# Bringing the late edges to their columns as three bf16 digits: one step of a graph attention and expert kernel on one Trainium2 core

## The chip, the core and the metric

The kernel runs on one core of one Trainium2 chip. The time is the device time of one execution in microseconds. The core's engines run side by side, each in its own order: TensorE (PE; PEld is its weight load), VectorE (DVE), ScalarE (ACT), GpSimd (POOL) and SyncE (SP, which issues DMA). Where one needs another's result it waits on a semaphore.

## The reference: what is computed

The program is a graph attention layer over 6250 nodes and 100,000 edges, followed by a feed-forward layer with eight experts of which each node uses one. Cut to what matters:

```python
# attention: x (6250, 256), 2 heads of 128
Wh = (layernorm(x) @ W_w + W_b).reshape(N, 2, 128)
s, t = Wh . a_src, Wh . a_dst                       # one number per node and head
e = leaky_relu(s[src] + t[dst], 0.2)                # one number per edge and head
alpha = softmax of e over the edges of one src
x = x + segment_sum(alpha * Wh[dst], src)           # Wh where a node has no edge
# experts: W1 (256, 1024), Wd (8, 1024, 256)
h = gelu(layernorm(x) @ W1 + b1)
probs = softmax(h @ Wg + bg); pick the best expert e of each node
x = x + probs[e] * (h @ Wd[e] + bd[e])
```

The edges come unsorted by `src`, so each node's edges must first be found, and then the rows `Wh[dst]` fetched from memory.

## The kernel before

**Prologue (to about 114 us).** The edges are sorted as keys on DVE. A key holds the source node, the destination (13 bits, from bit 8) and the node's place in its block (the low 8 bits). PE projects the nodes (L456), and their rows go to a table in DRAM, which ACT's queue stores. POOL sets small constants at the start.

**Blocks.** The 6250 nodes are 49 blocks of 128 (`NB`), one node to a partition. Each block gathers its edges' rows as 14 columns (`T`) of 128 rows. Eight columns (`ND`) hold the first eight edges of each node directly. Edges beyond the eighth are the *late* edges: up to 32 per node (`NR`), packed over the block into 768 slots (`NS`), that is six more columns (`NC`). Edges to the most frequent destinations, the *hot* pairs, go another way, without a gather.

The steps of one block b that matter here:

- `window`: POOL fetches each node's stretch of sorted keys (L619) into `win`.
- `measure`: DVE counts each node's edges; ACT makes `over`, the number of late ones (L640).
- `prefix`: PE adds `over` up over the partitions (L650). `prefix_out`: ACT copies the result to `late` (L653): a node's first slot in column 0, the slot after its last in column 2. It copies the first slot to the last column of `rest` as well (L655).
- `split`: DVE takes the window apart. The late keys (21 bits of each) become fp32 numbers in `rest`, 2^23 plus the bits (L659). `pick` is 1 where a slot (of 768) belongs to the node (L662, L663). L666 to L674 make the places and pairs.
- `gather_late`: six PE products (L738) of `pick`, 128 slots at a time, with `rest`, 33 columns. Each slot has one node, so the product brings that node's 32 late keys and its first slot to the slot.
- `choose`: DVE subtracts the first slot from the slot's number (L745), so knows which of the 32 keys is the slot's, takes it (L747 to L751), and cuts destination and place out of its bits (L753, L755, and L756 on ACT).
- `spread` transposes the places (PE L761, ACT L763), and SP sends them through DRAM (`lrow`) back to all partitions (`lbc`). `compare` (DVE L771) and `factors` (PE L779) make the attention's source factors from it.
- `fetch`: POOL issues the 14 gathers of table rows (L792), in three groups.
- `compare_back` (DVE L809), `weigh` (DVE L821 to L823, ACT L824 and L826) and `add_up` (PE L833) give each row its weight and add the rows of a node up in PSUM. `finish` (DVE) divides.

**Expert phases.** After every four blocks the feed-forward layer runs for their nodes: hidden layer (PE L920, ACT L922), choice of expert, turned rows (PE L1043, ACT L1044 and L1059) that POOL sends to their expert (L1064), and expert products (PE L1154).

**The order** is written out by hand. Each step is put with `at(slot, place, step, block)`, three slots to a block (`u = 3 * b`). The plan is sorted by slot and place, and each engine runs its instructions in the order in which the sorted steps issue them. Several blocks are under way at a time: a block's `split` stands at slot u-3, its `fetch` from u on, its `add_up` from u+3 on. `split` stands at place 12 of its slot, `weigh` of another block at place 8.751, `gather_late` at 33.7.

Of the kernel before, what the change touches and what calls it, by code (L numbers as in the profile page):

```python
# [10 lines left out]
F32 = mybir.dt.float32  # L11
BF16 = mybir.dt.bfloat16
I32 = mybir.dt.int32
U16 = mybir.dt.uint16
AF = mybir.ActivationFunctionType
ALU = mybir.AluOpType
# [7 lines left out]
P = 128  # L24
# [12 lines left out]
def common_path(  # L37
# [22 lines left out]
    nc = tc.nc  # L60
# [19 lines left out]
    HB, HK = 2, 4  # L80
    HOT = HB * P
    ND, NC, WIN = 8, 6, HK + 40
    NR = WIN - HK - ND
    KS = ES + WIN
    NS = NC * P
# [25 lines left out]
    const = ctx.enter_context(tc.tile_pool(name="const", bufs=1))  # L111
# [47 lines left out]
    first = const.tile([P, NB + 1], I32, name="first")  # L159
    minus_nd = const.tile([P, 1], F32, name="minus_nd")  # L160
    nc.gpsimd.memset(minus_nd, float(-ND))
    iota_bf = const.tile([P, HOT], BF16, name="iota_bf")
    nc.vector.tensor_copy(iota_bf, iota_s[:, :HOT])

# [3 lines left out]
    late = const.tile([P, NB, 3], F32, name="late")  # L168
# [4 lines left out]
    bias = const.tile([P, C], F32, name="bias")  # L173
# [20 lines left out]
    with ExitStack() as edges:  # L194
# [3 lines left out]
        def at(slot, place, fn, *args):  # L198
            plan.append((slot, place, len(plan), fn, args))

        kp = edges.enter_context(tc.tile_pool(name="keyp", bufs=2))
# [122 lines left out]
        bufs = [None] + [keyb if i % 2 == 0 else keya[:, :ES] for i in range(len(steps))]  # L324
# [204 lines left out]
        for f0, f1, t0, step in ((n0, n1, 8.0, 0.7), (n4, NB - 1, 15, 2.0)):  # L529
            for j, b in enumerate(range(f0, f1)):  # L530
                c = b % CH
# [81 lines left out]
        win, kept, rows, own, sums, res = {}, {}, {}, {}, {}, {}  # L613
# [37 lines left out]

        def prefix_out(b):
            nc.scalar.copy(late[:, b, :], kept[b].pop("po"))  # L653
            rest = kept[b]["rest"] = kp.tile([P, NR + 1], F32, name="rest")
            nc.scalar.copy(rest[:, NR:], late[:, b, 0:1])  # L655

        def split(b):
            w = win.pop(b)
            nc.vector.tensor_scalar(kept[b]["rest"].bitcast(I32)[:, :NR], w[:, HK + ND:], 0x1FFFFF, 0x4B000000,  # L659
                                    op0=ALU.bitwise_and, op1=ALU.bitwise_or)  # L660
            pick = kp.tile([P, NS], F32, name="pick", bufs=1)
            nc.vector.tensor_scalar(pick, iota_s, late[:, b, 0:1], None, op0=ALU.is_ge)  # L662
            nc.vector.scalar_tensor_tensor(pick, iota_s, late[:, b, 2:3], pick, op0=ALU.is_lt, op1=ALU.mult)  # L663

            place_i = kp.tile([P, HK + ND], I32, name="place_i")
            nc.vector.tensor_single_scalar(place_i, w[:, :HK + ND], 255, op=ALU.bitwise_and)  # L666
            loc = kp.tile([P, T], F32, name="loc", bufs=5)
            nc.vector.scalar_tensor_tensor(loc[:, :ND], iota_r[:, :ND], cnt[:, b:b + 1], place_i[:, HK:],
                                           op0=ALU.is_lt, op1=ALU.mult)

            hot_i = kp.tile([P, HK], I32, name="hot_i")
            nc.vector.tensor_single_scalar(hot_i, w[:, :HK], 8, op=ALU.logical_shift_right)
            pair = kp.tile([P, HK], F32, name="pair")
            nc.vector.tensor_scalar(pair, hot_i, float(0x400000 + (b << 13)), None, op0=ALU.subtract)  # L674
            kept[b].update(loc=loc, pick=pick, pair=pair, place=place_i)

        def pick_pairs(b):
            pair, place_i = kept[b].pop("pair"), kept[b].pop("place")
            d, p = kept[b]["both"] = [kp.tile([P, HK, w], BF16, name=n, bufs=1) for n, w in (("dests", HOT), ("places", P))]
            for r in range(HK):  # L680
                nc.vector.tensor_scalar(d[:, r, :], iota_bf, pair[:, r:r + 1], None, op0=ALU.is_equal)  # L681
            nc.vector.tensor_tensor(p, iota_bf[:, P:2 * P].unsqueeze(1).to_broadcast([P, HK, P]),
                                    place_i[:, :HK].unsqueeze(2).to_broadcast([P, HK, P]), op=ALU.is_equal)
# [49 lines left out]
        def gather_late(b):  # L733
            k = kept[b]
            k["pm"] = ps2.tile([P, 512], F32, name="pm")
            pk = k["pm"][:, :NC * (NR + 1)].rearrange("p (c r) -> p c r", c=NC)
            for c in range(NC):
                nc.tensor.matmul(pk[:, c, :], k["pick"][:, c * P:(c + 1) * P], k["rest"], start=True, stop=True)  # L738

        def choose(b):  # L740
            k = kept[b]
# [182 lines left out]
        def blocks_of(k):  # L924
            return range(max(0, (k - 1) * FB + 1), min(NB, k * FB + 1))
# [272 lines left out]
        for b in range(NB):  # L1198
            u = 3 * b
            at(u + -6, 64.258, window, b)  # L1200
            at(u + -4, 24, measure, b)
            at(u + -4, 50.755, prefix, b)
            at(u + -3, 5, prefix_out, b)
            at(u + -3, 12, split, b)
            at(u + -3, 33.7, gather_late, b)
            at(u + -2, 62.758, pick_pairs, b)
            at(max(u + -1, -0.2), 63, load_terms, b)
            at(u + 1, 18.756, scale_terms, b, 0)
            at(u + 2, 4.751, scale_terms, b, 1)
            at(u + 0, 51.019, count_pairs, b)  # L1210
            at(u + 2, 51, weigh_pairs, b)
            at(u + 4, 51.256, add_pairs, b)
            at(u + -2, 16, choose, b)
            at(u + -2, 33.5, spread, b)
            at(u + 0, 9, compare, b)
            at(u + 0, 33, factors, b)
            at(u + 1, 47, factor_sums, b)
            at(u + 5, 42.752, owned, b)
            at(u + 6, 13, owned_biased, b)
            for q in range(3):  # L1220
                at(u + 0 + q, 30, fetch, b, q)
                at(u + 1 + q, 51.259, compare_back, b, q)
                at(u + 2 + q, 8.751, weigh, b, q)
                at(u + 3 + q, 32, add_up, b, q)
            at(u + 6, 14, finish, b)

        worked = n_off = 0
        u = [3 * blocks_of(k)[-1] + 6 for k in range(NPH)]
# [57 lines left out]
@with_exitstack  # L1286
def gat_then_ffn_kernel(
    ctx: ExitStack,
    tc: tile.TileContext,
    x: bass.AP,  # L1290
    src: bass.AP,
    dst: bass.AP,
    W: bass.AP,
    Wb: bass.AP,
    a: bass.AP,
    W1: bass.AP,
    b1: bass.AP,
    Wg: bass.AP,
    bg: bass.AP,
    Wd: bass.AP,  # L1300
    bd: bass.AP,
    out: bass.AP,
):
    keep = ctx.enter_context(tc.tile_pool(name="keep", bufs=1))
    odd = keep.tile([1, 1], I32, name="odd")
    common_path(tc, x, src, dst, W, Wb, a, W1, b1, Wg, bg, Wd, bd, out, odd)
    flag = tc.nc.values_load(odd[0:1, 0:1], min_val=0, max_val=1,
                             skip_runtime_bounds_check_because="a flag, 0 or 1")
    with tc.If(flag > 0):
        general_path(tc, x, src, dst, W, Wb, a, W1, b1, Wg, bg, Wd, bd, out)  # L1310
# [506 lines left out]
```

## Time and profile before

| | us |
|---|---|
| median of 3 runs | 1271.98 (1270.6 to 1276.46) |
| the profiled execution | 1270.99 |
| its span, first to last instruction | 1268.9 |
| PE busy | 1108.0 (87%) |
| DVE busy | 969.4 (76%) |
| ACT busy | 677.6 (53%) |
| POOL busy | 835.5 (66%) |
| mean granted PE clock | 0.948 of full speed |

The profile is of one execution. A group's line gives line, engine, operation, the tiles out<-in, and a count; after the bar busy time and the mean of one in ns; after the next bar the idle time of the engine just before these instructions and what ended it. `issue` is idle time for which the profile shows no release. A timeline line begins with start and duration in us, with the idle time before it in brackets. A chain line has start, duration and the work; a line of waits has the total, how often, and the longest. "Slices" are 40 equal parts of the span, a digit being busy tenths. L numbers are lines of the kernel before.

### The profile page before, as it was taken

To read this page: it belongs to the slowest core of one execution; us is meant where nothing else is said; L and a number is where in the kernel's file an instruction comes from. 1 tells how busy PE (TensorE), PEld (TensorE's weight loads), DVE (VectorE), ACT (ScalarE), POOL (GpSimd) and SP (SyncE) were. 2 spreads that over 40 slices of the span, in tenths; PEclk is the share of its full clock that TensorE was granted. 3 is DMA by queue.
4 is the path that set the end of the run, shared out by engine and by line. 5 is a ranking of instruction groups with operands and counts; after the bars stand their busy time and mean duration, and the time that the engine had idled before them with its cause. 6 is when DMAs were issued, how large, how long until landed. Compare 5 with 4: busy or idle time off the path is not lost.

```text
span 1268.9 us, 22698 instructions
## 1 busy us (share of the span) xinstructions
PE 1108.0 (87%) x6551; PEld 864.0 (68%) x6551; DVE 969.4 (76%) x3509; ACT 677.6 (53%) x2011; POOL 835.5 (66%) x941
## 2 busy tenths in 40 slices
PE   4685677697888989999989999999999999999994
PEld 3464565566566677786876867868678687685784
DVE  6986889888979789798897997979979979753110
ACT  4684344555646447556474665655745647555221
POOL 1003777777777777777777777777777777736551
PEclk9797688898998989999999999999999999999998
DMA  4764776656555666666766666575667566747860
GB/s 142 220 196 137 200 199 207 192 190 200 173 173 176 218 172 214 190 223 197 216 191 217 212 195 206 183 241 177 222 187 227 183 211 187 230 138 298 318 202 13
DMA packets 115977, 249.77 MB, mean 197 GB/s; under 512 B 23372, under 2 KB 69656, under 8 KB 115702
## 3 DMA queue, kind: packets, MB, share of 16 engines
q0 software_dynamic: 44192, 131.04, 33.3%
q1 hardware_dynamic: 64342, 110.14, 27.3%
q10 hardware_dynamic: 7312, 7.05, 1.7%
q8 instruction: 56, 0.92, 0.3%
q14 instruction: 75, 0.61, 0.2%
HBM read 196.90 MB, written 57.97 MB: 201 GB/s over the span
## 4 chain that ended last, share of the span: by engine, by line
PE 42%; DVE 25%; DMA 12%; ACT 10%; issue 5%; POOL 4%; SPq 0%; ACTq 0%; DVEq 0%; POOLq 0%
PE pf L1154 11%; PE p_a L833 10%; PE pf L920 9%; DMA wg<-table,dsti 7%; POOL wg L792 3%; DVE wg L823 3%; PE pm L738 3%; DVE hot L809 3%; PE pf L1043 2%; ACT wg L826 2%; DMA lbc<-lrow 2%; DVE pick L663 2%; PE pf L456 1%; PE p_a L717 1%; DVE dests L681 1%
## 5 line engine op out<-in xcount | busy, mean ns | idle before, releaser
L792 POOL DMA_INDIRECT wg<-table,dsti x686 | 672.8, 981 | 211.4 <-issue 162.5
L833 PE MATMUL p_a<-wg,hot 128*128 128x258 f32 x1372 | 339.8, 396 | 0.0
L833 PEld LDWEIGHTS p_a<-wg,hot 128*128 128x128 f32 x1372 | 265.9, 198 | 57.4 <-issue 17.9
L826 ACT ACTIVATE wg<-wg 128x128 f32<-128x128 f32 x686 | 216.7, 390 | 4.8
L1154 PE MATMUL pf<-wd_sb,half 128*128 x880 | 205.6, 387 | 1.1
L1154 PEld LDWEIGHTS pf<-wd_sb,half 128*128 128x128 f32 x880 | 163.3, 191 | 31.4 <-ACT half L1044 5.5
L920 PE MATMUL pf<-xT,w_sb 128*128 128x512 f32 (+1 forms) x416 | 182.4, 584 | 0.5 <-ACT xT L912 0.5
L824 ACT COPY wg<-fix 128x10 f32<-128x10 f32 x147 | 24.1, 164 | 224.9 <-DVE wg L823 188.6
L920 PEld LDWEIGHTS pf<-xT,w_sb 128*128 128x128 f32 x416 | 75.3, 196 | 73.3 <-issue 69.2
L1044 ACT COPY half<-pf 128x512 f32<-128x512 f32 x110 | 59.1, 588 | 115.2 <-PE pf L1043 115.2
L823 DVE TENSOR_TENSOR wg<-wg,fix 128x640 f32<-128x640 f32 x147 | 114.1, 776 | 5.1
L809 DVE TENSOR_TENSOR hot<-fix,loc 128x640 f32<-128x640 f32 x147 | 112.7, 767 | 0.0
L738 PE MATMUL pm<-rest,pick 128*128 128x33 f32 x588 | 82.3, 295 | 15.1 <-DVE place_i L666 15.0
L738 PEld LDWEIGHTS pm<-rest,pick 128*128 128x128 f32 x588 | 77.8, 211 | 16.0 <-ACT wg L826 9.8
L922 ACT ACTIVATE hT<-pf,b_sb 128x512 f32<-128x512 f32 (+1 forms) x104 | 65.7, 655 | 29.4 <-PE pf L920 28.3
L456 PE MATMUL pf<-w_sb,xT 128*128 128x260 f32 x196 | 61.6, 443 | 19.1 <-ACT xT L450 19.0
L1064 POOL DMA_INDIRECT by_expert<-row,place_i x47 | 48.4, 1030 | 37.4 <-ACT row L1059 19.9
L704 ACT ACTIVATE wt<-tm,hot_e 128x128 f32<-128x128 f32 x196 | 67.8, 395 | 0.0
L619 POOL DMA_INDIRECT win<-keys,first x49 | 46.9, 958 | 28.9 <-DMA keys<-keyb 12.0
L821 DVE TENSOR_TENSOR fe<-fs,wg 128x10 f32<-128x10 f32 x147 | 24.1, 164 | 53.9 <-DMA wg<-table,dsti 50.1
L1043 PE MATMUL pf<-ident,hT 128*128 128x128 f32 x392 | 54.4, 278 | 10.7 <-ACT row L1044 5.4
L456 PEld LDWEIGHTS pf<-w_sb,xT 128*128 128x128 f32 x196 | 38.6, 219 | 28.7 <-ACT xT L450 24.3
(273 smaller groups left out, 1800.1 us busy)
## 6 DMA issues: line engine op xcount, KB each, us to landing
row<-by_expert SPq DMA_DIRECT2D x39, 641.0 KB
lbc<-lrow SPq DMA_DIRECT2D x49, 448.0 KB
wg<-table,dsti POOLq DMA_INDIRECT x686
wg<-by_expert SPq DMA_DIRECT2D x16, 641.0 KB
wd_sb<-in_L_ffn_Wd_dram SPq DMA_DIRECT2D x8, 1024.0 KB
tm<-terms SPq DMA_DIRECT2D x49, 128.0 KB
table<-tb ACTq DMA_DIRECT2D x12, 520.0 KB
xs<-in_x_dram SPq DMA_DIRECT2D x12, 512.0 KB
```

Of the source, the lines that this page charges most:

```text
L456: nc.tensor.matmul(pW[:, :TW], xT[:, k * P:(k + 1) * P], w_sb[:, k, :], start=(k == 0), stop=(k == KC - 1))
L704: nc.scalar.activation(kept[b]["wt"][:, g, h, :], tm[:, h, :], AF.Identity, scale=hot_e[:, g, 1, h:h + 1])
L738: nc.tensor.matmul(pk[:, c, :], k["pick"][:, c * P:(c + 1) * P], k["rest"], start=True, stop=True)
L792: nc.gpsimd.indirect_dma_start(out=wg[:, t - QS[q], :], out_offset=None, in_=table[:, :], in_offset=bass.IndirectOffsetOnAxis(ap=kept[b][" ...
L809: nc.vector.tensor_tensor(hot[:, :n], iota_ps.unsqueeze(1).to_broadcast([P, n, P]), kept[b]["loc"][:, QS[q]:QS[q + 1]].unsqueeze(2).to_bro ...
L823: nc.vector.tensor_mul(wg[:, :, :D], wg[:, :, :D], p_w[:, :, 0:1].to_broadcast([P, n, D]))
L826: nc.scalar.activation(wg[:, t, D2:SE], wg[:, t, D2:SE], AF.Identity, scale=wg[:, t, D + 1:D2])
L833: nc.tensor.matmul(sums[b], hot[:, t - QS[q], :], wg[:, t - QS[q], :SE], start=(t == 0), stop=(t == T - 1))
L920: nc.tensor.matmul(ph[:, :w], wt["w1"][:, k, j * P:(j + 1) * P], xT[:, k, :w], start=(k == 0), stop=(k == KC - 1))
L922: nc.scalar.activation(hT[:, j, :w], ph[:, :w], AF.Gelu, bias=wt["b1"][:, j:j + 1])
L1043: nc.tensor.transpose(pT[:, j * P:(j + 1) * P], rows(4 * h + j), ident)
L1154: nc.tensor.matmul(py[:, :C], res[k]["half", i, j // 4][:, j % 4, :], wt["wd"][:, ds(of * KH + j * C, C)], start=False, stop=(j == KH - 1))
```

## The change

The late keys no longer go to their slots as one fp32 number but as three bf16 numbers. DVE takes the three digits (bits 0 to 7, 8 to 15, 16 to 20) out of the key as integers in one instruction, where L659 made the fp32 number. ACT turns them to bf16 in a new step `rest_digits`, placed right behind `split`, and adds 2^23 to the third. Each digit is exact in bf16, and so is the third with 2^23. The first slot is given as a bf16 number and a bf16 remainder; the remainder is one more ACT instruction in `prefix_out`. `pick` is bf16. `gather_late` runs three bf16 products for each of the six columns of slots and lets PSUM add them up, so that `choose` finds the same numbers as before. The place numbers in the plan are the same but for the new step.

In all, per block: PE 18 bf16 loads and products for 6 fp32 products; ACT three instructions more; DVE as many as before; SP nothing; POOL four memsets more, once.

```diff
+    digits = const.tile([P, 3, NR], I32, name="digits")
+    for i, m in enumerate((0xFF, 0xFF00, 0x1F0000)):
+        nc.gpsimd.memset(digits[:, i, :], m)
+    two23 = const.tile([P, 1], F32, name="two23")
+    nc.gpsimd.memset(two23, float(1 << 23))
...
         def prefix_out(b):
             nc.scalar.copy(late[:, b, :], kept[b].pop("po"))
-            rest = kept[b]["rest"] = kp.tile([P, NR + 1], F32, name="rest")
-            nc.scalar.copy(rest[:, NR:], late[:, b, 0:1])
+            rest = kept[b]["rest"] = kp.tile([P, 3, NR + 1], BF16, name="rest")
+            nc.scalar.copy(rest[:, 0, NR:], late[:, b, 0:1])
+            nc.scalar.activation(rest[:, 1, NR:], rest[:, 0, NR:], AF.Identity, scale=-1.0, bias=late[:, b, 0:1])
 
         def split(b):
             w = win.pop(b)
-            nc.vector.tensor_scalar(kept[b]["rest"].bitcast(I32)[:, :NR], w[:, HK + ND:], 0x1FFFFF, 0x4B000000,
-                                    op0=ALU.bitwise_and, op1=ALU.bitwise_or)
-            pick = kp.tile([P, NS], F32, name="pick", bufs=1)
+            parts = kept[b]["parts"] = kp.tile([P, 3, NR], I32, name="parts")
+            nc.vector.tensor_tensor(parts, w[:, HK + ND:].unsqueeze(1).to_broadcast([P, 3, NR]), digits,
+                                    op=ALU.bitwise_and)
+            pick = kp.tile([P, NS], BF16, name="pick", bufs=1)
...
+        def rest_digits(b):
+            parts, rest = kept[b].pop("parts"), kept[b]["rest"]
+            nc.scalar.copy(rest[:, :2, :NR], parts[:, :2, :])
+            nc.scalar.activation(rest[:, 2, :NR], parts[:, 2, :], AF.Identity, bias=two23)
...
         def gather_late(b):
...
             for c in range(NC):
-                nc.tensor.matmul(pk[:, c, :], k["pick"][:, c * P:(c + 1) * P], k["rest"], start=True, stop=True)
+                for i in range(3):
+                    w = NR + (i < 2)
+                    nc.tensor.matmul(pk[:, c, :w], k["pick"][:, c * P:(c + 1) * P], k["rest"][:, i, :w],
+                                     start=(i == 0), stop=(i == 2))
...
-            at(u + -3, 12, split, b)
+            at(u - 3, 12, split, b)
+            at(u - 3, 12.1, rest_digits, b)
```

## The prediction

> **What bounds the kernel now.** I read the shares and slices first, then the chain that ended last, then the idle time of each engine, because the first two disagree about who sets the pace.
>
> ```profile
> PE 1108.0 (87%) x6551; PEld 864.0 (68%) x6551; DVE 969.4 (76%) x3509; ACT 677.6 (53%) x2011; POOL 835.5 (66%) x941
> POOL 1003777777777777777777777777777777736551
> ...
> PE 42%; DVE 25%; DMA 12%; ACT 10%; issue 5%; POOL 4%; SPq 0%; ACTq 0%; DVEq 0%; POOLq 0%
> ...
> L738 PE MATMUL pm<-rest,pick 128*128 128x33 f32 x588 | 82.3, 295 | 15.1 <-DVE place_i L666 15.0
> ```
>
> PE is busiest and holds 42% of the chain, L738 (the products that change) 3% of it. But POOL's row of slices is flat: 7 in every full slice from 127 to 1110 us. So I asked for POOL's own groups between 114.8 and 1118 us (after the bar: busy time, mean ns of one, then the idle time before them):
>
> ```profile
> L792 POOL DMA_INDIRECT wg<-table,dsti x686 | 672.8, 981 | 211.4 <-issue 162.5 <-DMA wg<-table,dsti 10.4 <-PE p_a L833 8.8
> L619 POOL DMA_INDIRECT win<-keys,first x47 | 44.9, 954 | 14.3 <-issue 6.4 <-DVE st L862 1.5 <-DVE fix L822 1.2
> L1064 POOL DMA_INDIRECT by_expert<-row,place_i x41 | 42.6, 1039 | 15.8 <-ACT row L1059 3.5 <-issue 3.5 <-ACT row L1044 2.5
> L892 POOL MEMSET idle<- 1x1 f32 x20 | 4.0, 202 | 0.1
> ```
>
> Busy and idle add to 672.8+211.4+44.9+14.3+42.6+15.8+4.1 = 1005.9 us, the whole stretch of 1003. The gathers' idle is 211.4/686 = 0.31 us each. The timeline shows what it is, and where POOL really waited:
>
> ```profile
> 807.73 0.95 POOL L792 DMA_INDIRECT wg<-table,dsti  x1 [0.30 <-issue]
> 810.80 1.10 POOL L1064 DMA_INDIRECT by_expert<-row,place_i  x1 [2.12 <-ACT wg L824]
> 811.90 0.09 POOL L892 MEMSET idle<- 1x1 f32 x1
> 812.20 1.36 POOL L1064 DMA_INDIRECT by_expert<-row,place_i  x1 [0.21 <-ACT wg L826]
> ```
>
> Each gather is 0.95 us and a pause of 0.30, whoever is named for it. So POOL issues back to back for 1002 us, and that is the pace. Over 0.30 it waited only at five sends (L1064, starting at 475.9, 479.6, 726.1, 810.8 and 975.0), by 0.3+2.3+1.45+1.8+0.5 = 6.4 us. The last gather ends at 1117.2, its sum (L833) at 1132.2; the rest is the last FFN, which the change doesn't touch. PE has slack inside the pace: from 480 to 1080 us its listed waits total some 28 us, 15.1 of them on one line:
>
> ```profile
> PE pf L650 <- ACT over L640: 15.1, 8, 2.2
> ```
>
> **The change part by part.** The sum is made against the profiled execution: 1270.99 us, a span of 1268.9 and 2.1 around it. It lies 0.99 below the median of three, 1271.98.
>
> *Products (L738, 49 blocks).* Removed: six fp32 products, in the chain as 12 passes:
>
> ```profile
> 1085.41 0.33 PE pm L779 x14
> 1085.74 1.36 PE pm L738 x12
> 1087.11 0.45 PE pm L691 x8
> ```
>
> Added: 18 pairs of a bf16 load and a bf16 product, 33 columns (32 for the third digit). No such pair is in the trace; the neighbours bound it. Fourteen pairs with 6 columns take 0.33 us, 24 ns each: 0.42 for 18. Eight with 128 columns take 0.45, 56 ns each: 1.01. At 33 columns I interpolate 24+32×27/122 = 31 ns, 0.56 us. Saved per block: 1.36-0.56 = 0.80 us (0.35 to 0.94), 39 us of PE in all (17 to 46). At half clock L738 takes 2.74 and saves about twice that.
>
> *What the saving is worth.* Counted by the chain it would be large: about 25 of the 49 blocks' products lie on it, for some 20 us of savings. I don't take this: while POOL issues back to back, an earlier product only makes PE wait longer. Two places can give something. First, the five sends wait for rows that PE and ACT make; the most is 6.4 us. The least is negative, because ACT gets more work ahead of those rows (below). I take 2.5 us, a little under half, since most of these waits name ACT. Second, the tail. PE runs without a gap from 1079.5 to after 1132, with one L738 in it (1085.74): 0.8 us. The part before 1079.5 begins with a wait on ACT. DVE's only wait on L738 nearby is 2.5 us at 1028, so the tail may give up to 3.3; I take 1.2.
>
> *ACT, three more instructions per block.* One in prefix_out behind L655 (so ahead of the next L824), two (rest_digits) behind a weigh's L826. No row has their forms; the nearest are the small copies L655 (191 ns), L756 (193) and L763 (247): 0.2+0.25+0.25 = 0.7 us, 34 us in all (0.5 to 0.9 per block). ACT is busy 53% and waits 186 us at L824 for DVE alone, so as throughput this is covered. As delay: behind rest_digits on ACT stand row copies (L1044, L1059) that L1064 waits for. Five sends later by 0.7 cost 3.5 us at most; that is in the 2.5 just taken.
>
> *ACT's new wait.* rest_digits waits for the DVE op that makes the parts, which stands behind the compare L771 on DVE; in the timeline near 810 the op in that place (L659) ends at 811.1, while ACT's five L826 run to 812.2. So normally there is no wait. L771 waited for its DMA 9 times, 14.9 us in all: then ACT waits too, and behind it the hidden-layer activations L922, L1044, and the next L824. PE's new wait for the digits costs at most 0.45 us a block against the 3.3 us per 82 that it is already idle. I price both at nothing; without the cover it is at most 14.9 us.
>
> *DVE.* L659 (32 elements, 236 ns) becomes a two-input op over 96; between L745 (6 elements, 155 ns) and L747 (192, 359) it is about 255, so +0.02, 1 us in all (-2 to +6). The pick's first op (L662, 628 ns for 768 f32) now writes bf16: 628 again, or at L809's time per element (815 ns for 640) 0.98, 17 us in all. The second (L663) already takes 1.02 us, and with a bf16 input I leave it. DVE is 84% busy from 115 to 1117 and waits 50 us for gathered rows; this hides there.
>
> *POOL and SP.* Four memsets before the sort. Rows of POOL memsets are 0.09 to 0.2 us: at most 0.8 us, hidden by a wait of 4.2 us for the destinations' load on the way to the sort. SP gets no instruction; its lrow and lbc transfers start when L763 is done, at most 0.7 us later. No gather is moved.
>
> *Contention.* L663 is a DVE op with two SBUF inputs. Some of the gathers beside it are long:
>
> ```profile
> 608.67 1.37 POOL L792 DMA_INDIRECT wg<-table,dsti  x1 [0.30 <-DMA wg<-table,dsti]
> ```
>
> Of 735 gathers and windows 66 exceed 1.06 us, 24 us in all over 0.945. Gathers that overlap L663 are on average 0.16 us longer. The new parts op, also with two inputs, has a quarter of its length: 0.04×49 = 2 us at most if it acts alike, nothing if not; pick in bf16 could give back as much. I take +0.5 us.
>
> [...]
>
> Sum: 1270.99 - 2.5 - 1.2 + 0.5 + 0.2 (DVE in the tail's blocks) = 1268.0 on the profiled execution, 1269 beside the median. I give 1268.5.
>
> **The rivals.**
> *R1, PE pays in full (faster).* If the 0.30 us pauses hide waits on PE, or the gathers' start is released by it, the chain's 20 us come back: 1251. Against it: 685 of 686 pauses are 0.30 under every name. A weaker form: all 6.4 us of sends, 3.3 of the tail: 1270.99-9.7 = 1261; for it: the sends' rows are made by PE products.
> *R2, POOL is blocked by the new DVE work (slower).* As POOL is the pace, each lengthened gather adds directly. With the gains above halved to 1.8, L663's own 0.16 us once a block gives 1271.0+7.8-1.8 = 1277, just inside; the whole 0.255 of the parts op in every block gives 12.5-1.8 = 10.7 more, 1281.7. It decides from (6.4+1.8)/49 = 0.17 us a block. For it: POOL has no slack and the parts op is of L663's kind; against it: L747, also with two SBUF inputs and longer (359 ns), has no long gathers beside it.
> *R3, PE's clock falls.* In the slices PEclk is 8 or 9; stretches at half clock are 3.4 us long and follow PE waits near 2 us (at 665.9 and 915.0), while other waits that long kept full clock. The change adds 0.8 us of idle per block. Each extra stretch costs at most 1.7 us of PE. It shows only when PE's slack, 3.3+3.2 us per 82, is used up: four stretches per phase, 1.7 us each beyond. One in the tail is +1.7: 1270.
>
> [...]
>
> *R4, the products don't get shorter.* If the pair takes 56 ns as at L691, 0.35 per block is saved, and the sends keep their waits: 1271, still no change.
>
> **How the numbers follow.** A median of three here spans 0.46%, so 0.5%, 6.4 us, is about what tells from no change. Forecast and R3, R4, within 0.5% (1265.6 to 1278.3): 0.47, of which R3 and R4 have 0.12. R1 0.31: most of it in the weaker form around 1261 to 1265, 0.07 near 1251. R2 in its upper part, with lbc's late transfers on ACT (14.9 less the gains, 1282) beside it, 0.22; its lower part counts to the forecast. The range leaves out the full R1 below and R2's upper end: 1256 to 1281.
>
> **What would show each step.** PE's busy time at the new products 0.5 to 0.6 us per block instead of 1.36, and PE's idle time larger by some 35 us; POOL's last gather ending near 1115; waits at L1064 below 6.4 us in all; gathers still 0.95+0.30; three ACT rows near 0.2 us; no more half-clock stretches than before. Wrong: a last gather before 1108 (R1: POOL was not the pace), gathers with a mean above 1.00 us or many above 1.06 (R2), pauses above 0.30, or a DVE row of the parts or picks longer by over 0.3.

## The result, and the profile after

The changed kernel takes 1270.24 us (median of 14 runs, 1267.04 to 1274.04), the kernel before 1270.98 in as many runs beside it (1267.56 to 1278.0). The ratio is 0.9989, with a 95% interval of 0.9972 to 1.0007: no change that can be measured. In us the interval is -3.6 to +0.9.

PE did lose work, and its share of the chain fell. First lines of the page of the changed kernel: busy times, slices of POOL and of the granted PE clock, the chain by engine.

```profile
PE 1080.3 (85%) x6845; PEld 826.6 (65%) x6845; DVE 971.1 (76%) x3509; ACT 707.5 (56%) x2158; POOL 842.8 (66%) x945
...
POOL 1003777777777777777777777777777777746551
PEclk9697687897898999999999999998999999999997
...
PE 34%; DVE 32%; DMA 14%; ACT 7%; issue 6%; POOL 5%; DVEq 0%; ACTq 0%; POOLq 0%; SPq 0%
```

PE fell by 27.7 us and its share of the chain from 42% to 34% (in the second profiles, below, 37% and 35%). POOL's row is as flat as it was. Line numbers are 5 to 16 higher than before: the products are L752, the gathers L807, the sends L1079 (POOL's transfers of rows to their expert), the sums L848, the two pick instructions L669 and L670.

The products became as cheap as the cheap end of the bounds. In the chain near 1089 us, with the same neighbours as in the prediction:

```profile
1089.11 0.33 PE pm L794 x14
1089.43 0.47 PE pm L752 x18
1089.90 0.46 PE pm L703 x8
```

Eighteen pairs take 0.47 us where twelve passes took 1.36. Busy time of the products alone, 114 to 1117 us, in the kernel before and then in the changed one (PE, then PEld, then the granted clock):

```profile
114.00:1117.00 1003.00, 82.33 (x588) 77.83 (x588) 0.95 0.65 199
```
```profile
114.00:1117.00 1003.00, 30.94 (x882) 26.49 (x882) 0.93 0.64 199
```

That is 51.4 us less. All of PE in the stretch of the gathers, before and after:

```profile
115.00:1117.00 1002.00, 901.58 (x5557) 703.92 (x5558) 840.29 (x3028) 557.12 (x1666) 762.97 (x794) 0.95 0.65 200
```
```profile
115.00:1117.00 1002.00, 871.91 (x5840) 664.85 (x5840) 840.49 (x3025) 583.65 (x1803) 766.31 (x791) 0.93 0.64 199
```

Only 29.7 us became idle. In this slightly shorter stretch the products alone took 81.6 and 30.9 us, 50.7 less; the other 21.0 went to PE's remaining work, which was the same and took longer (841.0 us instead of 819.9), at a lower clock.

POOL's groups between 114.8 and 1120 us in the changed kernel:

```profile
L807 POOL DMA_INDIRECT wg<-table,dsti x684 | 676.4, 989 | 208.7 <-issue 166.7 <-PE p_a L848 9.4 <-DMA wg<-table,dsti 8.9
L624 POOL DMA_INDIRECT win<-keys,first x48 | 45.7, 952 | 17.8 <-issue 5.2 <-DVE parts L666 3.5 <-DVE st L877 1.5
L1079 POOL DMA_INDIRECT by_expert<-row,place_i x41 | 45.6, 1111 | 13.3 <-issue 4.9 <-ACT wg L839 2.1 <-ACT row L1074 1.3
L907 POOL MEMSET idle<- 1x1 f32 x20 | 2.4, 122 | 0.0
```

The sends wait less (13.3 us of idle, 15.8 before), but in this profile sends and gathers themselves take longer: means of 1111 and 989 ns instead of 1039 and 981. That is the trade which the experiments look into.

### The profile page after: what moved, and what is told of

Its sections match the earlier page's. It is cut to its first block, busy times and chain, and to the rows that moved or that the text cites. A ratio compares the mean times of both kernels' runs of the same rounds, so it can differ in the third digit from the quotient of the medians.

```text
span 1272.2 us, 23275 instructions
## 1 busy us (share of the span) xinstructions
PE 1080.3 (85%) x6845; PEld 826.6 (65%) x6845; DVE 971.1 (76%) x3509; ACT 707.5 (56%) x2158; POOL 842.8 (66%) x945
## 4 chain that ended last, share of the span: by engine, by line
PE 34%; DVE 32%; DMA 14%; ACT 7%; issue 6%; POOL 5%; DVEq 0%; ACTq 0%; POOLq 0%; SPq 0%
DMA wg<-table,dsti 10%; PE pf L1169 9%; PE pf L935 8%; PE p_a L848 8%; POOL wg L807 4%; DVE wg L838 4%; DVE hot L824 3%; PE pf L1058 2%; DVE pick L670 2%; PE p_a L729 2%; DVE dests L693 1%; ACT wg L841 1%; DVE pick L669 1%; DVE lbc L786 1%; DVE res L874 1%
## 5 line engine op out<-in xcount | busy, mean ns | idle before, releaser
L807 POOL DMA_INDIRECT wg<-table,dsti x686 | 678.3, 989 | 209.3 <-issue 167.3
L848 PE MATMUL p_a<-wg,hot 128*128 128x258 f32 x1372 | 340.1, 397 | 0.0
L848 PEld LDWEIGHTS p_a<-wg,hot 128*128 128x128 f32 x1372 | 267.1, 199 | 57.3 <-issue 18.8
L838 DVE TENSOR_TENSOR wg<-wg,fix 128x640 f32<-128x640 f32 x147 | 114.1, 776 | 5.1
L824 DVE TENSOR_TENSOR hot<-fix,loc 128x640 f32<-128x640 f32 x147 | 112.7, 767 | 0.0
L1079 POOL DMA_INDIRECT by_expert<-row,place_i x47 | 51.4, 1093 | 32.6 <-ACT row L1074 15.1
L1058 PE MATMUL pf<-ident,hT 128*128 128x128 f32 x392 | 57.4, 289 | 10.2 <-ACT row L1059 5.6
L1059 ACT COPY row<-pf 128x512 f32<-128x512 f32 x94 | 51.0, 582 | 18.1 <-PE pf L1058 18.1
L729 PE MATMUL p_a<-hot_x,wt 128*128 128x129 f32 x392 | 60.9, 306 | 0.0
L729 PEld LDWEIGHTS p_a<-hot_x,wt 128*128 128x128 f32 x392 | 56.4, 221 | 1.3
```

The source lines that it names most:

```text
L729: nc.tensor.matmul(sums[b][:, hs], wt[:, g, h, :], hot_x[:, g, hs], start=False, stop=False)
L807: nc.gpsimd.indirect_dma_start(out=wg[:, t - QS[q], :], out_offset=None, in_=table[:, :], in_offset=bass.IndirectOffsetOnAxis(ap=kept[b][" ...
L824: nc.vector.tensor_tensor(hot[:, :n], iota_ps.unsqueeze(1).to_broadcast([P, n, P]), kept[b]["loc"][:, QS[q]:QS[q + 1]].unsqueeze(2).to_bro ...
L838: nc.vector.tensor_mul(wg[:, :, :D], wg[:, :, :D], p_w[:, :, 0:1].to_broadcast([P, n, D]))
L848: nc.tensor.matmul(sums[b], hot[:, t - QS[q], :], wg[:, t - QS[q], :SE], start=(t == 0), stop=(t == T - 1))
L1058: nc.tensor.transpose(pT[:, j * P:(j + 1) * P], rows(4 * h + j), ident)
```

## The experiments

Every ratio is to the kernel before on the same chip. My theory was that POOL's gathers are the pace and PE's saving is therefore worth next to nothing. The rival was that the saving pays, and that something the change brings (lengthened gathers, a lower clock) takes it back.

**Second profiles of both kernels.** The two first profiles differed by several us in places that need not have to do with the change, so I took each again, with no edit.

> The kernel before once more, for a second profile. The first had its first gather at 114.9 us, a gather stream of 1002.3 us, 22.7 us of gather time over the median gather (8.9 of it beside the second pick instruction, 24 long gathers) and two half-clock stretches after 480 us. If the differences between the two profiles (7.2 us more long-gather time, four more half-clock stretches after the change) come from the change, this profile repeats these numbers within about 2 us and one stretch. If they are chance from execution to execution, they move here by as much.

> The changed kernel once more. The first profile: gather stream 1007.0 us, 29.9 us of long-gather time, 49 long gathers beside the second pick instruction, sends waiting 3.0 us, tail from the last gather to the last sum 12.3 us, six half-clock stretches after 480 us. If the change causes them, they repeat; if chance, long-gather time anywhere from 20 to 32 us and a span nearer 1268, since that execution (1274.0) was the slowest of 14.

They took 1272.61 and 1272.46 us. From each trace I worked out the same figures. "Long" is the time of POOL's 774 gathers, windows and sends over 0.945 us each; "beside pick" is the part of it in those that overlap the second pick instruction; "waits" is what POOL waited beyond its pauses of 0.30; "tail" runs from the last gather's end to the last sum; the last column counts the half-clock stretches of 3.4 us from 480 us to the last gather. The other kernels in the table come below.

| | first gather | stream | long | beside pick | waits | tail | half clock |
|---|---|---|---|---|---|---|---|
| before | 114.9 | 1002.3 | 29.0 | 10.3 | 6.4 | 15.0 | 2 |
| before again | 113.6 | 1005.0 | 34.1 | 12.3 | 4.2 | 15.1 | 1 |
| changed | 115.9 | 1007.0 | 37.3 | 18.7 | 3.3 | 12.3 | 7 |
| changed again | 114.6 | 1004.0 | 35.3 | 17.2 | 2.3 | 15.0 | 8 |
| products three times (pe3) | 116.7 | 1001.3 | 33.2 | 15.4 | 1.6 | 14.9 | 1 |
| parts behind the picks | 115.5 | 1000.5 | 33.5 | 12.6 | 0.6 | 15.2 | 8 |
| one-input picks | 115.0 | 995.6 | 28.4 | none | 0.6 | 12.6 | 3 |
| the same, with filler | 115.6 | 997.3 | 26.1 | none | 4.5 | 16.5 | 2 |

Three things repeat in these two pairs: the changed kernel has more half-clock stretches (7 and 8 against 2 and 1), more long-gather time beside the second pick (17 to 19 against 10 to 12), and shorter waits. The length of the tail doesn't repeat. The kernel before moved by 5 us in long-gather time between its own two profiles, more than the 2 us that I had allowed for. And the profiled executions of the changed kernel lie 3.8 and 2.2 us above its median; those of the kernel before are within 2 us of its own.

**The products three times over.** PE's work is put back, nothing else.

```diff
-            for c in range(NC):
+            for c in [*range(NC)] * 3:
                 for i in range(3):
```

> The changed kernel with every one of the 18 small products run three times over: 54 load and product pairs at 25.5 ns, 1.38 us per block, which is what the six fp32 products took; 45 us of PE put back, nothing else changed. Theory POOL is the pace: the time stays that of the changed kernel, 1.000 to 1.003 of before, PE busy rises by some 45 us or a little less, and the half-clock stretches fall back to about two. Rival that PE's saving pays and something else (long gathers, clock) takes it back: slower than the changed kernel by 0.3% or more, up to 20 us (1.016).

Measured: 1271.9 us, 1.0002 (0.9985 to 1.002). Products, then all of PE, in its profile:

```profile
114.00:1117.00 1003.00, 77.10 (x2646) 72.65 (x2646) 0.96 0.66 200
```
```profile
115.00:1117.00 1002.00, 891.93 (x7614) 695.39 (x7615) 841.93 (x3032) 587.48 (x1814) 766.77 (x794) 0.96 0.66 200
```

With 46 us more of products, PE as a whole is busy only 20 us longer: its other work takes 814.8 us instead of 841.0, the clock rises from 0.93 to 0.96, and one half-clock stretch is left of seven. Against the changed kernel the time is 0.13% longer, with an uncertainty of 0.25% from the two intervals: PE's saving is worth at most some 5 us, and most likely 2 or less. The full 20 us of the chain's count are excluded; the low end of the rival's range, 0.3%, is not.

**No two-input pick.** The second pick instruction reads the slot numbers and the first one's result, two SBUF tensors. Here a comparison with one input makes a second tile, and PE subtracts it by twice the products. In this kernel `parts` also has one buffer instead of two.

```diff
-            nc.vector.scalar_tensor_tensor(pick, iota_s, late[:, b, 2:3], pick, op0=ALU.is_lt, op1=ALU.mult)
+            past = kp.tile([P, NS], BF16, name="past", bufs=1)
+            nc.vector.tensor_scalar(past, iota_s, late[:, b, 2:3], -1.0, op0=ALU.is_ge, op1=ALU.mult)
...
-                for i in range(3):
+                for i in (1, 2, 0):
...
+                    for m in ("pick", "past"):
+                        nc.tensor.matmul(pk[:, c, :w], k[m][:, c * P:(c + 1) * P], k["rest"][:, i, :w], ...)
```

> The changed kernel without the second pick instruction, which reads two SBUF tensors. In its place a second one-input comparison (slot past the node's last, times -1) makes a tile of its own, and PE adds the products of both tiles: 36 pairs per block, about 0.92 us, instead of 18. Theory that the long gathers beside the second pick instruction cost POOL time: they go, 10 to 18 us less, 0.986 to 0.992 of before, long-gather time near 12 us. Rival that gathers are lengthened whatever DVE runs then: long-gather time stays 25 to 30 us and the time 0.998 to 1.002; if one-input comparisons in fp32 block POOL as well, the same. DVE has 0.4 us per block less to do, which POOL as the pace would not show.

Measured: 1264.9 us, 0.9943 (0.9922 to 0.9965); against the changed kernel 0.46% less, with an uncertainty of 0.28%. The instruction of 1018 ns became one of 615, and POOL's groups (113.5 to 1120 us) read:

```profile
L809 POOL DMA_INDIRECT wg<-table,dsti x686 | 673.3, 981 | 209.1 <-issue 171.3 <-DMA wg<-table,dsti 8.2 <-PE p_a L850 7.9
...
L1081 POOL DMA_INDIRECT by_expert<-row,place_i x41 | 41.8, 1020 | 8.7 <-ACT late L658 2.7 <-ACT wg L841 1.9 <-issue 1.7
```

Gathers and sends are shorter and the sends wait less: with all 686 gathers counted, 678.3+45.6+13.3 us (677.0+44.9+11.6 in the second profile) became 673.3+41.8+8.7. But long-gather time fell by 7 to 9 us, not by the 17 to 19 that stood beside the instruction: other DVE instructions, now at other times, lengthened gathers in its place. The gathers that start during the comparison into `places` (L694, here L695) and the maximum over `wt` (L721, here L722) lost 17.4 us here, 11 to 13 in the changed kernel's profiles. By size the expectation was too high.

**The same with DVE's time given back.** Was it the second input, or the 0.4 us per block that DVE saved?

```diff
+            nc.vector.tensor_scalar(pick[:, :480], iota_s[:, :480], late[:, b, 0:1], None, op0=ALU.is_ge)
```

> The kernel without a second pick instruction of two SBUF inputs, which was 0.9943 of before, with its gain in DVE time given back: a one-input comparison over 480 numbers, about 0.41 us, is added behind the two, so DVE is as busy as in the changed kernel. Theory that gathers were lengthened by the two-input instruction: the gain stays, 0.992 to 0.996. Rival that the gain was DVE's 0.4 us per block (20 us in all): it goes, 0.997 to 1.001. Since all that DVE does later moves by 0.4 us against the gathers, the lengthening by other instructions may move by some 3 us either way.

> The kernel without a two-input pick instruction and with 0.41 us of one-input filler on DVE, again on another chip, for the same reason. By the theory that the two-input instruction lengthened gathers, the gain stays: 0.992 to 0.996 of before, long-gather time 22 to 26 us. By the rival that the gain was DVE's time, it goes: 0.997 to 1.001.

The first of these runs fell on a chip on which the kernel before took 1719 us (below). The second: 1267.35 us, 0.9954 (0.9932 to 0.9976). DVE is busy 970.8 us, as in the changed kernel (971.1), and most of the gain is there: 0.46% below the kernel before, 0.57% without the filler, a difference within the intervals. So the instruction with two inputs is what cost time, through POOL's gathers, and not DVE's load.

That instruction is also the longest of its block, so the runs alone do not show that it is the second input that counts. The traces say more. Take, in the two profiles of each kernel, the gathers that start while a DVE instruction still has 0.3 us or more to run. During the second pick there are 59, longer by 0.47 us on the mean and by 0.34 at least. During two others with both inputs in SBUF, the comparison into `places` (L682, now L694) and the maximum over `wt` (L709, now L721), there are 57 and 48, longer by 0.43 and 0.29. During `compare_back` (L809, now L824) there are 278, and none is longer by more than 0.02, though it too has two inputs and runs 0.67 to 0.82 us. One of its inputs, `fix`, lies in PSUM. The same holds of L823 (now L838): of 171 such gathers 18 are over 0.1 us longer, all of them where L771 (now L786) comes next on DVE. One case of L809 in the kernel before, DVE and then POOL:

```profile
599.42 0.81 DVE L809 TENSOR_TENSOR hot<-fix,loc 128x640 f32<-128x640 f32 x1
```
```profile
599.90 0.95 POOL L792 DMA_INDIRECT wg<-table,dsti  x1 [0.30 <-ACT hT L922]
```

Two inputs in SBUF are not the whole of it: the comparison L771 (now L786), which has one large input, in bf16, lengthened 23 of 38 such gathers by over 0.1 us.

**Parts behind the picks.** The same instructions in another order.

```diff
-            parts = kept[b]["parts"] = kp.tile([P, 3, NR], I32, name="parts")
-            nc.vector.tensor_tensor(parts, ...)
             pick = kp.tile([P, NS], BF16, name="pick", bufs=1)
             nc.vector.tensor_scalar(pick, iota_s, late[:, b, 0:1], None, op0=ALU.is_ge)
             nc.vector.scalar_tensor_tensor(pick, iota_s, late[:, b, 2:3], pick, op0=ALU.is_lt, op1=ALU.mult)
+            parts = kept[b]["parts"] = kp.tile([P, 3, NR], I32, name="parts")
+            nc.vector.tensor_tensor(parts, ...)
```

> The changed kernel with the parts instruction behind the two pick instructions on DVE instead of ahead of them; no work is added or left out. In four profiles the length of a gather beside the second pick instruction follows one curve of when that instruction starts after the gather's start, before the change and after it: about 0.40 us longer at -0.55 us, 0.50 at -0.45, 0.02 to 0.03 at +0.15, 0.08 to 0.11 at +0.25, 0.15 at +0.35. The change moved the starts some 0.1 us to the right, since the parts instruction takes DVE 0.16 us and L659 took 0.08. Theory of the phase: with 0.16 us taken off, the starts move left, past those of before; long-gather time beside it falls from 16 to 18 us to 9 to 11, and the time by 3 to 7 us, 0.993 to 0.998 of before. Rival that the bf16 form of the instruction is what lengthens gathers: nothing changes, 0.998 to 1.001.

> The kernel with the parts instruction behind the picks again, on another chip: on the first one the kernel before took 1719 us and POOL waited some 440 us beyond its pauses, so POOL was not the pace there and the run (1.0066) says nothing of gathers. The expectation is as it was: by the theory of the phase long-gather time beside the second pick instruction falls from 16 to 18 us to 9 to 11, and the time is 0.993 to 0.998 of before; by the rival that the bf16 form lengthens gathers, 0.998 to 1.001.

The phase that the expectations speak of can be seen in one block. POOL's timeline of the changed kernel, and DVE's beside it:

```profile
648.05 1.09 POOL L807 DMA_INDIRECT wg<-table,dsti  x1 [0.30 <-PE pf L1058]
649.44 1.43 POOL L807 DMA_INDIRECT wg<-table,dsti  x1 [0.30 <-issue]
```
```profile
648.20 0.25 DVE L666 TENSOR_TENSOR parts<-win,digits 128x96 int32<-128x96 int32 x1
648.36 0.61 DVE L669 TENSOR_SCALAR pick<-iota_s,late 128x768 bf16<-128x768 f32 x1
649.01 1.02 DVE L670 SCALAR_TENSOR_TENSOR pick<-iota_s,late,pick 128x768 bf16<-128x768 f32 x1
```

L670 starts 0.43 us ahead of the second gather, runs 0.59 us into it, and the gather takes 1.43 instead of 0.95. In the kernel before, the same block's L663 starts 0.12 us after its gather, and that one is hardly longer:

```profile
646.05 0.99 POOL L792 DMA_INDIRECT wg<-table,dsti  x1 [0.30 <-issue]
```
```profile
646.16 1.02 DVE L663 SCALAR_TENSOR_TENSOR pick<-iota_s,late,pick 128x768 f32<-128x768 f32 x1
```

On a chip like the first, the reordered kernel took 1270.75 us, 1.0 (0.9986 to 1.0015). The phase theory is half right: the time that it expected, 0.993 to 0.998, didn't come. Beside the second pick the long-gather time fell to 12.6 us, close to the level before the change though not to the 9 to 11 expected, and the starts lie near the same curve (-0.55 us: 0.33, where it was 0.34 to 0.41 in the others; -0.35: 0.50, where it was 0.50 to 0.52; +0.15: 0.01; +0.25: 0.12 us). So it is when the instruction runs that counts; the fp32 form of the kernel before lies on the same curve as the bf16 form. But the sum over all gathers stayed at 33.5 us, since the instructions behind the picks moved as well, and with it the time.

**ACT's new work four times over.**

```diff
+            for _ in range(4):
                 nc.scalar.copy(rest[:, :2, :NR], parts[:, :2, :])
                 nc.scalar.activation(rest[:, 2, :NR], parts[:, 2, :], AF.Identity, bias=two23)
```

> The changed kernel with the two new ACT instructions of rest_digits done four times over, 1.65 us more of ACT per block, 81 us in all. Theory that ACT's new work is hidden: 0.998 to 1.002 of before, ACT busy near 790 us; the sends of rows may wait some 1.5 us longer each where such a group stands ahead of them, up to 0.3% in all. Rival that ACT's order ahead of the sends is what takes the saving back: 3% or more of ACT time shows, 1.005 or slower, with the waits at the sends above 6 us.

Measured: 0.9979 (0.9924 to 1.0034), but on a chip where the kernel before took 1719 us. There ACT's work is hidden; for the others this run is only a hint.

**One more gather per block.**

```diff
+            if q == 0:
+                more = gp.tile([P, TW], F32, name="more", bufs=1)
+                nc.gpsimd.indirect_dma_start(
+                    out=more, out_offset=None, in_=table[:, :],
+                    in_offset=bass.IndirectOffsetOnAxis(ap=kept[b]["dsti"][:, 0:1], axis=0))
```

> The changed kernel with one more gather of table rows per block (the first column again, into a tile that nobody reads). Theory POOL is the pace: each takes its 0.95 us and pause of 0.30, 49 times 1.25 = 61 us, ratio 1.045 to 1.05. Rival that another engine sets the pace and POOL's stream is stretched to fit: less than half of that, under 1.024; if PE or DVE set it alone, 1.00 to 1.01.

> The changed kernel with one more gather per block, again on another chip, since on the first POOL was not the pace. Theory POOL is the pace: 49 times 1.25 = 61 us, 1.045 to 1.05 of before, with pauses still 0.30. Rival that another engine sets the pace: under 1.024.

Both runs fell on chips where the kernel before took 1719 and 1672 us, and gave 1.0525 (1.0455 to 1.0596) and 1.0727 (1.0647 to 1.0807), 90 and 122 us. On the second the kernel before itself ranged from 1665 to 1705 us. POOL wasn't the pace there (it waited 448 us and more beyond its pauses), so the direct test of the pace on an undisturbed chip is still missing.

**Parts by one-input instructions too.**

```diff
-            nc.vector.tensor_tensor(parts, w[:, HK + ND:].unsqueeze(1).to_broadcast([P, 3, NR]), digits, op=ALU.bitwise_and)
+            for i, m in enumerate((0xFF, 0xFF00, 0x1F0000)):
+                nc.vector.tensor_single_scalar(parts[:, i, :], w[:, HK + ND:], m, op=ALU.bitwise_and)
```

> The kernel with two one-input comparisons in place of the two-input pick instruction (0.9943 of before), and with the parts made by three one-input instructions of 32 elements, some 0.19 us each, instead of the one two-input instruction of 96; the digits constant is dropped. Theory that any two-input instruction lengthens gathers in proportion to its length: another 0.25 us of such time per block gone, 2 to 4 us, 0.990 to 0.994 of before. Theory of the phase alone: DVE's later instructions move some 0.1 us against the gathers, and the time stays 0.993 to 0.997, with the long-gather time spread otherwise over the instructions.

Measured: 1.0689 (1.0648 to 1.073) on the chip where the kernel before took 1672 us. It tells nothing of the parts instruction, but it is no small matter for the one-input picks. Of PE's waits on that kind of chip, in the kernel with filler (a twin of this one on PE; total, times, longest), and then in the one with the parts behind the picks, which has the changed kernel's products:

```profile
PE pm L755 <- issue: 260.7, 237, 2.6
```
```profile
PE pm L752 <- issue: 40.5, 40, 2.0
```

PE stands still at the small products with nothing that the profile shows to wait for, some 1 us at a time and up to 2.6. On the other chips PE has, during the gathers, no pause without a named wait of over 0.8 us in any profile; here it had some 120 to 210 on all lines together, 60 to 174 of them at products into the same tile, `pm`. The times fit: the kernel with filler, with twice the products, took 1.0459 (1.0413 to 1.0505) of before there, the reordered one 1.0066 (1.0029 to 1.0104). But no run there changed the number of products alone, and one more gather cost as much without any.

So the one-input picks beat both kernels where the kernel before takes 1271 us, and in the two forms that ran there (with filler, and with the parts split up) lose to the kernel before where it takes 1700.

## Why the prediction held, step by step

The forecast was no change, 1268.5 us with a range of 1256 to 1281 and 0.47 for "within 0.5%". Measured was 1270.24. The direction of the argument held: POOL is back to back (beyond its pauses it waited 3.3 and 2.3 us in streams of 1007.0 and 1004.0), so PE's saving goes to idle time. The time alone confirms little, since the range is 25 us wide, and the 3.0 us that the sum takes off lie inside the measured interval, and so does no change at all. What confirms the argument is the products three times over.

*Products.* Estimated at 0.56 us per block, between 0.42 and 1.01; measured 0.46, that is 25.4 ns a pair from start to start. The interpolation by columns was wrong, since 33 columns cost hardly more than 6 (25.2 ns). R4 is out.

*What the saving is worth.* Waits at POOL: 2.5 us less was predicted; over two profiles each the mean went from 5.3 to 2.8, which is 2.5. Tail: 1.2 predicted, 2.7 in the one pair of profiles and 0.1 in the other, so the term is not confirmed. R1 in full is excluded by the products three times over.

*Contention.* This is the term that looks mis-sized: +0.5 us predicted. Long-gather time was 29.0 and 34.1 us in the kernel before and 37.3 and 35.3 in the changed one, +4.8 on the mean, and the last gather ended at 1122.9 and 1118.6 us, not near 1115. But the kernel before varies by 5 us in the total on its own, and with the products three times over, the same gathers and the same DVE instructions, it was 33.2. So it is likely, and not shown, that this term took the rest of the gain.

The mechanism was only half named. I had priced the parts instruction as another blocker of L663's kind. What repeated was that the second pick, unchanged in length, lengthens gathers by 17 to 19 us (15.4 with the products three times over) instead of 10 to 12. The order of the instructions explains it: the parts instruction takes DVE some 0.08 us longer ahead of the pick, which starts later against the gather, and with the parts behind the picks it was 12.6 again.

R2 as a slower kernel didn't come: 0.17 us a block were needed, some 0.1 were there. The argument against it, that L747 has no long gathers beside it, does not hold over four profiles: five gathers start with 0.2 us or more of it to run, and four of these are 0.1 us longer.

The removal of the two-input pick bears the contention out: gathers' and sends' time fell by 7 to 9 us against the changed kernel. What makes such an instruction hold up a gather, no run shows.

*Clock (R3).* The prediction gave as its sign "no more half-clock stretches than before". That failed: 7 and 8 against 2 and 1, behind PE pauses of 0.9 to 2.8 us. Per stretch the price was about right: five more at 1.7 us are 8.5, and from 480 to 1117 us PE's other work took 10.8 us longer (seven more, 11.9, and 12.4 measured in the second pair). The rest of the 21.0 us lies before 480 and stays open. The effect on the time was priced right too. PE's idle time, 27.5 us from 480 to 1080 in the kernel before (3.8 per 82, not the 3.3 of the prediction), covers it, and the products three times over, with one stretch, were no faster. What PE now waits for (480 to 1080 us) shows who is late next; before and then after:

```profile
PE pm L761 <- ACT loc L756: 0.8, 3, 0.3
```
```profile
PE pm L776 <- ACT loc L771: 11.7, 11, 2.7
```

PE comes to the transpose earlier and stands there until ACT has the places from DVE. DVE in turn waits for gathered rows, 81.6 and 70.2 us in the two profiles (50.1 and 66.2 before); that this is what makes the places late is read from the order of the instructions.

*ACT.* Three rows of 0.7 us together (0.5 to 0.9) were estimated. They are:

```profile
L660 ACT CAST rest<-late x49: 193/193/195, 114.1 to 1083.6; 128x1 bf16<-128x1 f32 x49
L661 ACT ACTIVATE rest<-rest,late x49: 297/297/298, 114.3 to 1083.8; 128x1 bf16<-128x1 bf16 x49
L686 ACT CAST rest<-parts x49: 231/233/250, 114.5 to 1085.7; 128x64 bf16<-128x64 int32 x49
L687 ACT ACTIVATE rest<-parts,two x49: 317/318/323, 114.7 to 1085.9; 128x32 bf16<-128x32 int32 x49
```

The last three (the first replaces L655) sum to 0.85 us, and ACT is busy 29.9 us longer. ACT's wait for the parts came twice, 3.7 us in all, of 14.9 feared; PE waited for the digits once, 0.2 us.

*DVE.* Parts 251 ns (255 estimated), first pick 613 (628 taken, 980 the bound), second 1018 as before.

*POOL at the start.* The four memsets were called hidden. They seem not to be quite: the first instruction of the sort starts at 9.85 and 9.78 us, before at 9.62 and 9.56, some 0.2 us later. The first gather starts 1.3 us later on the mean (114.3 us in the two profiles of before, 115.6 in the six others of the table); no run shows what the rest of that is.

## What to carry to other kernels

Before a saving on the busiest engine is counted, look for one that issues back to back at a fixed beat, here POOL with 0.95 us and a pause of 0.30, and ask whether that beat depends on the saved work. Here it didn't: of the 50.7 us that the products gave up, 29.7 became PE's idle time, and 21.0 went to its other work, at a granted clock of 0.93 instead of 0.95. Where GpSimd's gathers are the pace, as here, look for long DVE instructions with two SBUF inputs that run across a gather's start before shortening PE: the one of 1018 ns lengthened the gathers that start during it by 0.47 us on the mean. Replacing one by one-input instructions gained 0.5% here, on chips like the first; to move one of its inputs to PSUM is what the traces suggest (beside L809, none of 278 gathers was longer by more than 0.02 us), and no run has tried it. A profile of one execution places such contention, but two of the same kernel are needed to know which of its numbers repeat.

## What the runs showed that I had not expected

- A gather's length follows when the two-input instruction of 1018 ns starts against it: started 0.45 us ahead, 0.42 to 0.49 us longer; started 0.15 us after, 0.03 at most. The gather seems to be held up until the instruction ends: where it starts during the second pick, it is longer by what the pick still has to run (0.55 to 0.62 us on the mean) less 0.12. The runs show the curve, not the mechanism.
- 33 columns cost PE 25.4 ns a pair, 6 columns 25.2.
- A DVE instruction with two inputs lengthened gathers where both lay in SBUF (0.29 to 0.47 us on the mean), and in none of 278 cases where one lay in PSUM (L809).
- PE at the same work was 21.0 us slower in 1002 when it had more idle time (22.8 in the second pair of profiles), and the granted clock went from 0.95 to 0.93; with the work put back it went to 0.96.
- On two of the chips the kernel before took 1672 and 1719 us. PE paused for 1 to 2 us at its small products without a named wait, and POOL waited for 430 us and more beyond its pauses. There the number of PE instructions may matter; why is open, and so is what the change itself does there, since it was not run alone on those chips.
